# A hybrid attention and state-space layer: its instructions ordered by the scheduler with another machine model

## The chip, the cores and the metric

The kernel runs on one core of a Trainium2 chip, as one program. The metric is the device time in microseconds (us); the runs of the kernel before gave 1927.61, 1928.0 and 1932.41 us, a median of 1928.0. A core has five engines, each of which works through its own list of instructions strictly in order: TensorE (PE, with its weight loads shown apart as PEld), VectorE (DVE), ScalarE (ACT), GpSimd (POOL), and SyncE (SP), which issues the kernel's DMA transfers. Engines wait for each other by semaphores. So what an instruction waits for is not only its inputs and its buffer, but also everything that stands ahead of it in its engine's list.

## The reference

Four layers, each added to the running value `x` (4 batches of 256 tokens, 512 features, all in fp32):

```python
x = x + attention(layernorm(x))       # 32 heads of 16, rotary, causal;
                                      # plus a gated attention to 10 adapter tokens
x = x + clustered_ffn(layernorm(x))   # dense = x @ weight.T + bias, kept only where ...
x = x + mixer(layernorm(x))           # state-space layer, below
x = x + clustered_ffn(layernorm(x))   # the same weights again
```

The clustered feed-forward takes `softmax(10 * x @ centroids.T)` over 64 clusters. A token is kept when any of its clusters exceeds 0.01; a feature is kept when its cluster is hit by any token of all batches. That last condition needs every token before any token can go on.

The mixer projects 512 features to 8192 gates, 8192 channels (128 heads of 64), B and C (8 groups of 128 each) and 128 time steps `dt`. Then:

```python
xBC = silu(causal_conv4(xBC) + conv_b)
y   = sum over j <= i of (C_i . B_j) * exp(cum_i - cum_j) * dt_j * x_j   # per head
g   = (y + D * x) * silu(gate)
g   = g * rsqrt(mean(g * g over the group's 1024 channels) + eps) * norm_w
out = g @ out_w.T
```

## The kernel before, in words

**Products in three parts.** [...]

**Attention** (about 0 to 385 us). Work is done in 32 units of 4 heads (8 units for each of the 4 batches). Of a batch, queries, keys and values are prepared in steps (`prepared`, L368's neighbourhood: normalise, project, rotate), and pieces of 8 heads are made (`stacked` L305 on POOL, transposes L380, copies L382). A unit then goes through four steps, one unit apart: `scores` (products L425 and a mask product L429, row maximum L434, exponentials L437), `turn` (transposes L452, copies L453), `weigh` (four products L462 and four L468 that each write 32 partitions of one bank `py`, copy L473), and `gathered` (L479, L485). At a batch's end come `closed` (L527, L530) and `ended` (L543). The first feed-forward (`Feed`, L170 on) runs in between, a token tile at a time, its last tiles behind attention.

**The step between the layers** (about 385 to 465 us). `select` makes the mask of features out of the hits of all tokens; `take` (L229) applies it; each of the 8 token tiles is normalised (`mxn`), transposed and split into `mx`, the mixer's input. The projection to `dt`, its softplus and its running sums in chunks of 128 tokens follow. The sums are written to HBM (`cumd`) and turned (`col_t`, `dt_t`).

**The mixer's blocks** (about 465 to 1853 us). 64 blocks of 128 channels (2 heads), 8 blocks to a group. A block i goes through these steps, in the order of the source:

- the projection of its channels, `pp` (128 x 1024, two banks of PSUM, two such buffers, L676), 24 products for block and gate each; its weights come as `wr` (three buffers, L684) and are split two projections ahead;
- `conv` (L839): ACT writes the accumulator from `pp` (L842), DVE adds three taps that read `pp` (L849), ACT applies silu (L853);
- for the block before: `product` (L917), 16 matmuls L923 into the one bank pair `pyy` (L675), and `gated` (L930): L933 and L936 on DVE, the spill to HBM (L938), squares on ACT (L943, L945) and their sum on POOL (L946);
- the gate's projection into the other `pp`, and its silu into `gt` (L1042; the one buffer of L1041);
- `differences` (L876) of the two heads: DVE L881, POOL's mask L885, on ACT eight exponentials of 128 x 128 (L890, L893) and one over four batches (L891), into `em` (three buffers, L878). They read the row of running sums `r`, which SP loads two heads ahead (L873, two buffers), and need the buffer that the `pyy` products of the block before read;
- `turned` (L899): transposes L908, DVE L909 into `xd`;
- `weighted` (L897): `em` times the masked C.B of the group, `gm`.

At a group's border B of the next group is projected in block 6 and C in block 7, each into a `pp` buffer like the others and each with its conv; then `scores` (L863, L867, mask product L868) makes the next `gm`. The output product of a group runs in the blocks of the next one: `recall` (L975) loads the spilled values and splits them (`gr`, `gh`), `out_weights` (L952) loads and scales the weights (`wor`, L955, L958, L959), `root` (L964) sums the squares on PE (`pqs`, L967) and takes the root on ACT (`rg`, L971), the products write `pog`, and `scaled` (L993) adds them to `x`. Thus the first group has no output products beside it, and each later group has 8 tiles of them.

The PSUM banks that are shared in turn by `trx`, `pg`, `pqs`, `pog` and others are the two buffers of tag `m` (L671).

**The end** (about 1853 to 1929 us): output products of the last group, the second feed-forward, the store.

**What sets the order.** The source gives no engine's list by hand. The body is traced once; every operation is recorded with its dependencies and buffers. A scheduler then plays the recorded program on a model of the machine: it keeps what is ready, gives each model engine its next instruction, and moves the model's clock on by the durations that the model has for it. The sequence in which this play issues the instructions becomes each engine's list on the chip. Pools of buffers (`bufs`) limit how far it runs ahead. `tc.keep_in_program_order` holds single instructions at their place in the source (L122, L955 and some in the transition); `tc.issue_after` puts the first two heads' exponentials behind the third silu. The order of one run is fixed when the program is built; nothing is reordered on the chip.

Of the kernel before, what the change touches and what calls it, by code (L numbers as in the profile page):

```python
# [21 lines left out]
B, L, C = 4, 256, 512  # L22
# [13 lines left out]
# Columns of the constant table.  # L36
# [12 lines left out]
def constants():  # L49
    """Masks, selections and rotary tables: they depend on the shapes alone."""  # L50
# [18 lines left out]
    # [token, token tile, queries or keys, cos or sin, term]  # L69
# [8 lines left out]
def hybrid_kernel(  # L78
# [23 lines left out]
    def split(hl, v, engine=nc.vector):  # L102
        """v as the sum of two parts that each fit the products' 12 bits."""
        nc.scalar.copy(hl[0], v)  # L104
        engine.tensor_tensor(hl[1], v, hl[0].bitcast(F32), ALU.subtract)  # L105

    def mm3(o, ls, rs, first=True, last=True):
        """o = the sum over k of ls[k].T @ rs[k], operands in two parts."""
        n = len(ls)
        for k in range(n):  # L110
            (lh, ll), (rh, rl) = ls[k], rs[k]
            nc.tensor.matmul(o, lh, rh, start=(first and k == 0), stop=False)  # L112
            nc.tensor.matmul(o, lh, rl, start=False, stop=False)  # L113
            nc.tensor.matmul(o, ll, rh, start=False, stop=(last and k == n - 1))  # L114

    def warmed(o, vs):
        """Products whose result nobody reads: they keep the array's clock up in a wait."""
        for v in vs:
            nc.tensor.matmul(o[:, : v.shape[1]], ones, v, start=True, stop=True)

    def primed(func):
        """Has the scalar engine load a function's table ahead of its use."""  # L122
# [3 lines left out]
    class Norm:  # L126
        """A layer's normalisation of x."""
# [32 lines left out]
        def turn(self, xn, tr, xs):  # L160
            """In two parts, features on partitions."""
# [4 lines left out]
        def turned(self, t, xn, tr, xs):  # L166
            """A token tile normalised, in two parts, features on partitions."""
# [4 lines left out]
    class Feed:  # L172
        """One clustered layer, a token tile at a time."""
# [22 lines left out]
        def tile(self, t, xs, halves):  # L196
            """What a token tile becomes where its columns are selected, and its hits."""
# [22 lines left out]
        def select(self, cnt, rows):  # L220
            """The columns of the clusters that any token hits, as a mask."""
# [10 lines left out]
    def attention(later):  # L232
        with ExitStack() as es:
# [40 lines left out]
            def rotated(pq, c, f, name):  # L274
                """Rotary embedding, tokens on partitions; f: 0 for queries, 1 for keys."""
# [14 lines left out]
            # Parts of 8 heads side by side so that one product of 48 terms carries  # L290
            # high * high + high * low + low * high.
# [19 lines left out]
            # Adapter keys and values, spread to block diagonals.  # L311
# [7 lines left out]
            def adapter_weights():  # L319
# [9 lines left out]
                for q in range(4):  # L329
# [4 lines left out]
                    # The heads' columns: two more to the right in each of the four products.  # L334
# [22 lines left out]
            def prepared(b):  # L357
                """Steps that make a batch's queries, keys and values."""
# [12 lines left out]
            def pieces(b, q):  # L371
                """Queries and keys of 8 heads, on partitions of (2 heads, 64 terms)."""
# [40 lines left out]
            def scores(b, u):  # L413
                """Softmax numerators of 4 heads, rows on partitions."""
# [41 lines left out]
            def weigh(b, u, eT):  # L456
                """Weighted values, on partitions of (head, 32), then turned and normalised."""
# [32 lines left out]
            def adapted(b):  # L490
                """Steps that make the adapter's part."""
# [31 lines left out]
            def closed(b, k):  # L523
                """A block of features of a batch, done and turned."""
# [139 lines left out]
    def mixer(feed, later):  # L664
        with ExitStack() as es, ExitStack() as inner:
# [21 lines left out]
            def prepare(i):  # L687
                """The halves of the projection's block i, in the order of use."""
# [83 lines left out]
            # dt, and the running sums of dt * A within chunks of 128 tokens.  # L772
            cumd = dram.tile([H, NT], F32, name="cumd")
            # What a key token's sums turn: minus its own in the first chunk, its own in the
            # second, and the way to the end of the first.
# [18 lines left out]
            # ln(1 + e) by its series where e is small.  # L794
# [13 lines left out]
            for half in range(2):  # L808
# [3 lines left out]
                # From each token of a batch's first chunk to the chunk's end.  # L812
# [26 lines left out]
            def conv(pp, ch, tag, bufs):  # L839
                """silu of the causal convolution of a block of channels."""  # L840
# [15 lines left out]
            def scores(bt, ct):  # L856
                """Masked C.B of a group, key tokens on partitions."""
# [18 lines left out]
            def differences(h, r):  # L876
                """The decay from key to query: zero where the key is behind the query."""
# [21 lines left out]
            def turned(n, x2):  # L899
                """x * dt of a block, tokens on partitions, in two steps."""  # L900
# [29 lines left out]
            def gated(n, x2, gt, py, sq):  # L930
                """(y + D x) * gate of a block, and its squares added up."""
# [20 lines left out]
            def out_weights(g, k):  # L952
                """A block of output weights times the norm's, in halves."""
# [21 lines left out]
            def recall(g, t, half):  # L975
                """A token tile of half of a group's blocks, in halves."""
# [20 lines left out]
            # A group's blocks: B and C of the next group come behind its own.  # L997
# [110 lines left out]
            for t in range(TT):  # L1108
# [7 lines left out]
                # The table for roots comes before the one for exponentials.  # L1116
# [18 lines left out]
def arrange(inputs):  # L1135
    """The inputs as the program reads them: rows reordered, axes turned, nothing computed."""
    f = {k[3:]: np.asarray(v) for k, v in inputs.items()}

    def turned(w):
        # [features, inputs] -> [input in block, block of inputs, features]  # L1140
# [15 lines left out]
    # [block, feature, input block, input] -> [block, input, input block, feature]  # L1156
# [47 lines left out]
```

## Time and profile before

| | |
|---|---|
| median of the runs | 1928.0 us |
| profiled execution, first to last instruction | 1929.2 us |
| PE busy / idle | 1882.0 us (98%) / 47 us |
| DVE, ACT, POOL busy | 1478.0 (77%), 1383.7 (72%), 346.0 us (18%) |
| DMA | 240.35 MB, mean 125 GB/s |
| mean granted TensorE clock | 0.989 of full speed |
| instructions | 29952 |

The span of the profiled execution is 1.2 us more than the median of the runs, and nothing lies around it: it is the execution's own time. In a group's line "idle before, releaser" is the engine's idle time in front of those instructions and what ended most of it. Windows of the trace give, for each engine, the busy time in a stretch with the number of instructions, then the clock granted to TensorE (1.00 is full speed), the share of time that DMA engines were busy, and GB/s. In a timeline each line is a run of like instructions: when it starts, how long it lasts, engine, source line, operation, tiles, and how many there are; a bracket at the end names an idle time ahead of it and its cause.

### The profile page before, as it was taken

How to read it: one execution, taken by the hardware profiler on the slowest of the kernel's cores; microseconds unless marked ns; L12 is line 12 of the kernel's file. 1: busy time of each engine (PE TensorE's matmuls, PEld its weight loads, DVE VectorE, ACT ScalarE, POOL GpSimd, SP SyncE). 2: the span in 40 equal slices, each digit the busy share in tenths (PEclk: the TensorE clock that was granted, in tenths of full speed). 3: DMA queues.
4: the chain of work that ended last, by engine and by line, in shares of the span. 5: the costliest groups of instructions: out<-in, count | busy, mean ns of one | idle time of the engine just before them, and what ended most of it. 6: DMA issues, size and time to landing. Idle time of an engine off the chain costs nothing.

```text
span 1929.2 us, 29952 instructions
## 1 busy us (share of the span) xinstructions
PE 1882.0 (98%) x10690; PEld 1470.6 (76%) x10690; DVE 1478.0 (77%) x2324; ACT 1383.7 (72%) x2873; POOL 346.0 (18%) x306
## 2 busy tenths in 40 slices
PE   7999999989999999999999999999999999999997
PEld 6767767767777777877787777777777777787786
DVE  5556557679998878877877797778777877877777
ACT  5665667557898677876877787778677877786753
POOL 4112120011231111122121111211111111121100
PEclk7999999989999999999999999999999999999999
DMA  4000000014555554555454455445444545455341
GB/s 140 1 1 1 1 22 24 12 38 153 166 193 182 158 166 146 154 153 164 152 164 149 154 164 160 149 144 181 148 164 151 160 157 159 133 169 158 117 126 48
DMA packets 151909, 240.35 MB, mean 125 GB/s; under 512 B 12368, under 2 KB 77520, under 8 KB 151760
## 3 DMA queue, kind: packets, MB, share of 16 engines
q1 hardware_dynamic: 151760, 238.44, 39.0%
q8 instruction: 84, 1.38, 0.3%
q14 instruction: 65, 0.53, 0.1%
HBM read 202.75 MB, written 35.65 MB: 124 GB/s over the span
## 4 chain that ended last, share of the span: by engine, by line
PE 83%; DVE 5%; ACT 5%; DMA 2%; issue 2%; SPq 0%; DVEq 0%; ACTq 0%
PE pp L112 12%; PE pp L114 12%; PE pp L113 11%; PE pyy L923 8%; PE pog L112 6%; PE pog L114 6%; PE pog L113 6%; PE sc L425 3%; PE trx L908 3%; PE ptr L452 2%; PE py L462 1%; DMA wor<-in_wout_dram 1%; PE sc L429 1%; PE trp L380 1%; DVE acc L849 1%
## 5 line engine op out<-in xcount | busy, mean ns | idle before, releaser
L112 PE MATMUL pp<-mx,w 128*128 128x512 f32 (+1 forms) x1160 | 469.1, 404 | 7.2 <-DVE acc L849 6.7
L114 PE MATMUL pp<-mx,w 128*128 128x512 f32 (+1 forms) x1160 | 459.0, 396 | 0.0
L113 PE MATMUL pp<-mx,w 128*128 128x512 f32 (+1 forms) x1160 | 458.1, 395 | 0.0
L849 DVE SCALAR_TENSOR_TENSOR acc<-pp,cw_s,acc 128x1012 f32<-128x1012 f32 (+2 forms) x240 | 304.8, 1270 | 23.7 <-ACT acc L842 23.1
L897 DVE TENSOR_TENSOR em<-em,gm 128x1536 f32<-128x1536 f32 x128 | 228.3, 1784 | 88.9 <-ACT em L891 80.6
L112 PEld LDWEIGHTS pp<-mx,w 128*128 128x128 f32 x1160 | 218.8, 189 | 68.3 <-issue 10.3
L114 PEld LDWEIGHTS pp<-mx,w 128*128 128x128 f32 x1160 | 218.6, 188 | 49.3 <-issue 0.4
L113 PEld LDWEIGHTS pp<-mx,w 128*128 128x128 f32 x1160 | 219.0, 189 | 45.1 <-issue 0.7
L946 POOL TENSOR_TENSOR sq<-sq,acc 128x1024 f32<-128x1024 f32 x55 | 132.6, 2411 | 584.0 <-ACT acc L945 584.0
L885 POOL TENSOR_SCALAR_AFFINE_SELECT r<-r 128x512 f32<-128x512 f32 x128 | 128.8, 1007 | 550.1 <-DMA r<-cumd 427.4
L104 ACT CAST w<-wr 128x512 fp32r<-128x512 f32 x144 | 88.5, 615 | 193.2 <-PE pp L113 169.9
L112 PE MATMUL pog<-wo,gh 128*128 128x512 f32 x512 | 204.2, 399 | 0.0
L114 PE MATMUL pog<-wo,gh 128*128 128x512 f32 x512 | 200.4, 392 | 0.0
L113 PE MATMUL pog<-wo,gh 128*128 128x512 f32 x512 | 199.7, 390 | 0.0
L890 ACT ACTIVATE em<-r,col_t 128x128 f32<-128x128 f32 x512 | 164.9, 390 | 48.3 <-PE pyy L923 46.9
L923 PE MATMUL pyy<-em,xd 128*64 128x256 f32 (+1 forms) x2048 | 188.7, 329 | 2.0 <-DVE em L897 1.9
L923 PEld LDWEIGHTS pyy<-em,xd 128*64 128x64 f32 x2048 | 133.1, 137 | 64.8 <-issue 21.1
L893 ACT ACTIVATE em<-r,col_t 128x128 f32<-128x128 f32 x512 | 166.4, 388 | 0.0
L881 DVE TENSOR_SCALAR em<-r,col_t 128x128 f32<-128x128 f32 x512 | 136.6, 326 | 11.8 <-PE pyy L923 10.1
L909 DVE TENSOR_TENSOR xd<-trx,dt_t 128x512 f32<-128x512 f32 x128 | 86.2, 683 | 61.6 <-PE trx L908 61.4
L105 DVE TENSOR_TENSOR w<-wr,w 128x512 fp32r<-128x512 f32 x139 | 98.0, 706 | 43.1 <-ACT w L104 42.4
L437 ACT ACTIVATE e<-sc,nmx 128x128 f32<-128x128 f32 (+1 forms) x256 | 105.4, 425 | 14.9 <-DVE nmx L434 14.8
(285 smaller groups left out, 3320.7 us busy)
## 6 DMA issues: line engine op xcount, KB each, us to landing
wr<-in_win_dram SPq DMA_DIRECT2D x287, 256.0 KB, 2.9
r<-cumd SPq DMA_DIRECT2D x128, 512.0 KB, 4.2
spill<-gb SPq DMA_DIRECT2D x63, 512.0 KB, 2.9
gr<-spill SPq DMA_DIRECT2D x120, 256.0 KB, 3.5
wor<-in_wout_dram SPq DMA_DIRECT2D x64, 256.0 KB, 3.1
out_dram<-x SPq DMA_DIRECT2D x8, 256.0 KB, 2.3
x<-in_x_dram SPq DMA_DIRECT2D x1, 1536.0 KB, 9.9
gr<-spill SPq DMA_DIRECT2D x8, 192.0 KB, 2.6
```

The source lines that it names most:

```text
L112: nc.tensor.matmul(o, lh, rh, start=(first and k == 0), stop=False)
L113: nc.tensor.matmul(o, lh, rl, start=False, stop=False)
L114: nc.tensor.matmul(o, ll, rh, start=False, stop=(last and k == n - 1))
L437: nc.scalar.activation(es_[c][:, 2 * j + pr, :], sc[:, j, :n], AF.Exp, bias=nm[:, j : j + 1], accum_out=rs[:, c, h : h + 1],)
L849: nc.vector.scalar_tensor_tensor(av[:, :, d:], pv[:, :, : L - d], cw_s[:, ch, tap : tap + 1], av[:, :, d:], ALU.mult, ALU.add,)
L881: nc.vector.tensor_scalar(e[:, b, 2, :], rv[:, b, 1, :], col_t[:, h, b, 1:2], 0.0, ALU.subtract, ALU.min,)
L885: nc.gpsimd.affine_select(rv[:, :, 0, :], rv[:, :, 0, :], pattern=[[0, B], [1, P]], compare_op=ALU.is_ge, fill=-1e30, base=0, channel_mult ...
L890: nc.scalar.activation(e[:, b, 1, :], rv[:, b, 1, :], AF.Exp, bias=col_t[:, h, b, 2:3])
L893: nc.scalar.activation(e[:, b, 0, :], rv[:, b, 0, :], AF.Exp, bias=col_t[:, h, b, 0:1])
L897: nc.vector.tensor_tensor(e, e, gm, ALU.mult)
L923: nc.tensor.matmul(py[d, b, k * P :], xd[:, 2 * b + k, d], es2[hh][:, b, 2 * k : 2 if k == 0 else 3, :].rearrange("p s i -> p (s i)"), sta ...
L946: (nc.gpsimd if n < NB - 1 else nc.vector).tensor_tensor(sq, sq, x2, ALU.add)
```

## The change

One argument of the context in which the kernel body is traced. It tells the scheduler to play the program on the machine of the timeline simulator instead of its default machine model. All computations, buffers, pools and pins stay as they are.

```diff
-    with tile.TileContext(nc) as tc:
+    with tile.TileContext(nc, schedule_with_timeline_sim=True) as tc:
         hybrid_kernel(tc, *args)
```

The rest of the diff takes comments and docstrings out, and leaves empty lines in their place, so that line numbers stay the same, for instance:

```diff
     def split(hl, v, engine=nc.vector):
-        """v as the sum of two parts that each fit the products' 12 bits."""
+
         nc.scalar.copy(hl[0], v)
```

Both programs can be set side by side before they run. They hold the same matmuls, vector operations and transfers; ACT has 195 table loads instead of 191, since the load for the silu of a block now stands ahead of L1042 in 48 places. The lists of all five engines differ. On PE, the 16 products L923 of a block stood together in 52 of 64 blocks and as 1 + 15 in 11; now they stand together in 14, as 8 + 8 in 36, and in other parts in 14. The four products L462 of an attention unit come in 32 runs instead of 55, those of L468 in 35 instead of 47, and the transposes L452 in 139 runs instead of 117. On ACT, 16 exponentials (those of both heads of a block) stand between a conv's start L842 and the next gate silu L1042 in 60 of 64 blocks; before, there were 14 to 16 in most blocks, and 8 in 14 blocks next to a group's border. On SP the loads of `wv` moved behind the large load of `x`, and up to six `wr` loads stand in a row ahead of an `r`. On POOL the mask operations L885 stand three and one around the sum L946 where they stood two and two.

## The prediction

> **What bounds the kernel now.** I read the page first, engine shares and then the costliest groups with the idle time in front of them:
>
> ```profile
> span 1929.2 us, 29952 instructions
> ...
> PE 1882.0 (98%) x10690; PEld 1470.6 (76%) x10690; DVE 1478.0 (77%) x2324; ACT 1383.7 (72%) x2873; POOL 346.0 (18%) x306
> ...
> L112 PE MATMUL pp<-mx,w 128*128 128x512 f32 (+1 forms) x1160 | 469.1, 404 | 7.2 <-DVE acc L849 6.7
> ```
>
> PE is busy 98% of the span: all its idle time is 47 us, so no order can gain more than that plus what PE wastes inside its own sequence. In the mixer its only repeated wait is a projection (`pp`) that waits for a convolution tap (L849), 6.7 us in all. Then the stretches (columns: length, PE, PEld, DVE, ACT, POOL busy with instructions, granted clock, DMA share, GB/s):
>
> ```profile
> 375.00:380.00 5.00, 2.91 (x19) 1.87 (x17) 3.75 (x13) 1.43 (x5) 0.00 (x0) 1.00 0.00 0
> 380.00:385.00 5.00, 4.61 (x15) 3.77 (x16) 0.67 (x2) 1.66 (x2) 0.00 (x0) 0.66 0.02 3
> ...
> 480.00:520.00 40.00, 38.26 (x222) 29.10 (x221) 39.15 (x50) 35.64 (x73) 9.39 (x8) 1.00 0.53 170
> ...
> 800.00:840.00 40.00, 40.00 (x220) 31.75 (x219) 30.68 (x41) 28.94 (x61) 6.21 (x5) 1.00 0.45 139
> ...
> 920.00:960.00 40.00, 39.15 (x215) 30.75 (x212) 34.31 (x46) 34.22 (x54) 4.31 (x3) 1.00 0.45 141
> ```
>
> In mid-group (800) PE never stops and ACT and DVE have a quarter of their time free. At a group's end (920) and in the first group (480, no output products yet) ACT and DVE are at 34 to 39 of 40: there the order decides. The timeline of ACT at a group's end shows the sequence that the change touches:
>
> ```profile
> 922.21 1.19 ACT L842 ACTIVATE acc<-pp,cb_s,cw_s 128x1024 f32<-128x1024 f32 x1
> 923.42 1.28 ACT L890 ACT_TABLE_LOAD   x1
> 924.71 1.28 ACT L890 ACTIVATE em<-r,col_t 128x128 f32<-128x128 f32 x4
> 925.90 0.68 ACT L893 ACTIVATE em<-r,col_t 128x128 f32<-128x128 f32 x2
> 926.48 1.05 ACT L945 ACTIVATE acc<-gb 128x1024 f32<-128x1024 f32 x1
> 927.43 0.68 ACT L893 ACTIVATE em<-r,col_t 128x128 f32<-128x128 f32 x2
> 928.13 1.28 ACT L1042 ACT_TABLE_LOAD   x1
> 929.42 1.03 ACT L1042 ACTIVATE gt<-pp 128x1024 f32<-128x1024 f32 x1
> ```
>
> Eight exponentials (L890, L893), those of one head, stand before the gate's silu (L1042), which frees a `pp` buffer. And PE there, with the one wait of 0.77 us:
>
> ```profile
> 919.71 2.55 PE L923 MATMUL pyy<-em,xd 128*64 128x256 f32 x30
> 922.20 0.50 PE L112 MATMUL pp<-mx,w 128*128 128x512 f32 x1
> ...
> 928.80 0.47 PE L112 MATMUL pp<-mx,w 128*128 128x512 f32 x1 [0.77 <-DVE acc L849]
> ```
>
> **The change part by part.** No instruction's work changes; each engine's list is reordered, SP's and POOL's too, and ACT gets 195 table loads for 191 (4 x 1.28, beside PE). I read the new order of each engine and costed it with rows of this trace; the sum starts at the profiled 1929.2 us, which lies 1.2 above the median of the runs.
>
> *Group ends, groups 2 to 8.* In the new order all 16 exponentials of a block stand between a convolution's start and the next gate silu in 60 of 64 blocks; before, it was 8 in 14 of the blocks at a group's border. At block 7 a third projection (C of the next group) follows at once and needs one of the two `pp` buffers. From the end of the x projection ACT has: cast 0.52, L842 1.21, table 1.29, 16 exponentials 4 x 1.19 = 4.76, two L891 1.08, cast 0.52, L945 0.95, table 1.29, L1042 1.03: 12.65. PE has 11 of the 16 `pyy` products (11/16 x 2.75 = 1.9, 0.4 around them) and 24 matmuls at 0.2325 (5.6): 7.9. Wait 4.7. The other buffer comes no sooner: the third tap now stands on DVE behind L881, L936 and an L897 (1.7). Everything of PE is behind this wait: C, the C.B products, the next block. Five groups show this sequence, one more place has 4.0: 27.5. The root of a group (L971) frees the bank that the first output product needs: ACT has 15 exponentials 4.4, three table loads 3.9, silu 1.0, root 0.3 = 9.6; PE has `pqs` 1.7, 24 matmuls 5.6, transposes and changes 0.7 = 8.0; wait 1.6, five times: 8. Taps: eight places of 0.9 to 1.8, because eight subtractions (0.19), L933 (1.19) and a mask product now lie between taps two and three: 9. Two places at C.B: 2. Together 46, less the 6 of before that they replace: **+40**.
>
> *First group and the dt stage (425 to 640).* No output products cover anything here and DVE is at 39 of 40. Three gate silus: 16 exponentials that wait for `pyy` to free `em` 4.76, L842 1.21, two L891 1.08, L943 0.95, table 1.29, L1042 1.03 = 10.3 against 3.2 of PE work: 7.1; the others 5.5 and 7.2. C.B: its mask product L868 stands on DVE behind the weights' L105, which waits for a cast behind two table loads and eight exponentials: 3.4; then behind L881, which waits for `r` (SP issues it behind a `wr`; 4.2 us to land, page): 3.0. `pyy` directly behind its transposes waits for L909 (2.4, 3.3, 0.9) and L897 (3.7, 1.2, 1.2). Taps 7.7. Together 48, less 4 of before: **+44**; bounds +15 (the gates alone, less what is there now) and +60.
>
> *PE's own sequence.* Before, 52 of 64 `pyy` groups run whole and 11 as 1 + 15; after, 14 whole, 36 as 8 + 8, 14 odd. A whole group takes 2.75 start to start, its batches 0.65 each, so each visit costs 0.15; a projection that starts again behind one 0.2. 117 visits for 76 and 191 projection runs for 179: 41 x 0.15 + 12 x 0.2 = **+9** (5 to 15). In attention it goes the other way: four products of L462 run side by side in 0.46, a lone one takes 0.55; before they come in 55 runs and L468 in 47 and take 41.4 us start to start, after in 32 and 35: 26.3. With 22 more runs of `ptr` transposes (0.09 each) and fewer of the rest: -16. Against it about 9 of new short waits (transposes of L380 eleven times behind their copies L382, `py` behind L473), since ACT and DVE are at two thirds there: **-7** (-16 to +5).
>
> *Start, transition, tail.* The interleaved queries and keys of two tiles save one 4 us wait for `axs`, a stack (POOL L306) costs 3 and 2, and `wv` moves on SP behind the 1.5 MB of `x` (9.9 us to land): -2 (-4 to +5). Between the layers five waits for `mxn` instead of three, more for `mx`: +6 (0 to 15). At the end `gh` and `x` 3, the count 1, the last group 1: +5 (0 to 8).
>
> *Clock.* Behind two idle stretches of 2.0 us in 377 to 380 the rows show 0.66 in the next 5 us: 1.7 us lost. Some 17 of the waits above are of 2 us or more. At the group ends the loss lets ACT catch up and eats the two later waits (1.1 + 1.6), so it costs nothing; of the 11 in the first group, 19 us, about half: **+8** (0 to 30). [...]
>
> The table load took 1.28 in every row here, and the next instruction started within 0.05. [...]
>
> Sum: 1929.2 - 2 - 7 + 6 + 44 + 40 + 9 + 5 + 8 = 2032, 2031 on the scale of the median. All low ends at once give about 1953, all high ends 2117.
>
> **The rivals.**
> - *Only the group ends wait.* The first group is DVE-bound already (39 of 40), so what PE waits there may be time that DVE would have cost anyway. Without the 44 and the 8: 1980. For it: PE waits only about 4 us there before although DVE is full. Against: DVE itself stands still 5.6 us in the C.B chain.
> - *The other side: the silu is in time.* If the 12.65 of ACT shrinks below 8.7 (7.9 plus the present 0.8), by fewer exponentials behind the x projection than the list shows because some ran during it, the group ends cost nothing, and attention's regrouping decides: 1929 - 16 + 9 - 2 = 1920, faster. Against: the exponentials of a block wait for `em` buffers that `pyy` frees after the x projection.
> - *The clock stays down.* The trace has one case where a 2.8 us idle is followed by 17 us at half clock (35 to 52 us). Five such at 8.5 us lost: 2032 + 43 - 8 = 2067 and more.
> - *It does nothing.* Excluded: the lists differ on every engine. Within 0.3% (6 us, about what a measurement of this kernel can tell) only by cancellation.
>
> **How the numbers follow.** Forecast 0.60 (1995 to 2060), only the group ends 0.20 (1960 to 1995), clock 0.13 (2060 to 2110), silu in time 0.05, cancellation 0.02. Predicted time 2031. Range 1976 to 2088: it cuts half of the second and third case and all of the last two. Faster 0.05, same 0.02, slower 0.93.
>
> **What would show it.** Right: `pp` waits for ACT `gt` L1042, some 45 us in 8 to 11 places, absent before; `pog` waits for ACT `rg`; PE idle near 150 us for 47; windows of half clock after 480 us; L462 only in fours; attention no longer than before. Wrong: if `pp` still waits for L849 alone with under 10 us, the chain of exponentials was covered; if attention ends over 15 us late, its short waits were undersized; if PE's idle is small and the time still long, the split `pyy` cost more than 0.15 a visit.

## The result, and the profile after

The changed kernel takes 2087.1 us (median of 4 runs, 2084.65 to 2087.44) against 1928.2 us before: the ratio is 1.081, with a 95% interval of 1.0794 to 1.0827. That is 159 us slower; the prediction said 103 slower, in a range that ends at 2088.

The head of the page of the changed kernel, and its group of projections, answer to the first lines shown of the kernel before:

```profile
span 2085.5 us, 29994 instructions
...
PE 1938.1 (93%) x10690; PEld 1505.2 (72%) x10690; DVE 1549.3 (74%) x2324; ACT 1385.8 (66%) x2877; POOL 403.3 (19%) x306
...
L112 PE MATMUL pp<-mx,w 128*128 128x512 f32 (+1 forms) x1160 | 478.0, 412 | 63.3 <-ACT gt L1042 51.9
```

L112, L113 and L114 are the three products that `mm3` makes of a pair of operands, each split in two by a cast (L104) and a subtraction (L105). PE's idle time went from 47 to 147 us, but its busy time also grew, by 56 us, with the same 10690 matmuls. The idle time ahead of L112 is now 63.3 us and most of it waits for the gate's silu L1042, where before it was 7.2 us and waited for a tap. The windows (columns as before) show what the busy time is made of:

```profile
480.00:520.00 40.00, 25.74 (x103) 18.94 (x104) 23.56 (x32) 23.87 (x49) 3.43 (x5) 0.71 0.32 106
800.00:840.00 40.00, 34.55 (x169) 26.77 (x164) 29.80 (x38) 27.19 (x53) 9.08 (x6) 0.91 0.43 136
920.00:960.00 40.00, 39.83 (x216) 30.75 (x215) 33.39 (x44) 30.31 (x58) 7.47 (x6) 1.00 0.46 148
```

In the first group PE is busy for 25.7 of 40 us, and the granted clock is 0.71 there; around a group's end (827 us) it is 0.91; only in mid-group, here 920 to 960, is it 1.00. A group's end on the three engines, PE first, then DVE, then ACT (timelines; the bracket is the idle time ahead and its cause):

```profile
827.08 0.40 PE L114 MATMUL pp<-mx,w 128*128 128x512 f32 x1
832.93 0.80 PE L112 MATMUL pp<-mx,w 128*128 128x512 f32 x1 [5.45 <-ACT gt L1042]
833.52 0.63 PE L113 MATMUL pp<-mx,w 128*128 128x512 f32 x1
```

```profile
826.62 1.27 DVE L849 SCALAR_TENSOR_TENSOR acc<-pp,cw_s,acc 128x1016 f32<-128x1016 f32 x1
828.58 1.76 DVE L897 TENSOR_TENSOR em<-em,gm 128x1536 f32<-128x1536 f32 x1 [0.69 <-ACT em L891]
830.26 1.27 DVE L849 SCALAR_TENSOR_TENSOR acc<-pp,cw_s,acc 128x1020 f32<-128x1020 f32 x1
```

```profile
820.73 1.20 ACT L842 ACTIVATE acc<-pp,cb_s,cw_s 128x1024 f32<-128x1024 f32 x1
821.94 1.28 ACT L890 ACT_TABLE_LOAD   x1
823.24 1.28 ACT L890 ACTIVATE em<-r,col_t 128x128 f32<-128x128 f32 x4
824.42 1.27 ACT L893 ACTIVATE em<-r,col_t 128x128 f32<-128x128 f32 x4
825.59 1.27 ACT L890 ACTIVATE em<-r,col_t 128x128 f32<-128x128 f32 x4
826.77 1.26 ACT L893 ACTIVATE em<-r,col_t 128x128 f32<-128x128 f32 x4
827.94 1.13 ACT L891 ACTIVATE em<-em 128x512 f32<-128x512 f32 x2
828.98 0.60 ACT L104 CAST w<-wr 128x512 fp32r<-128x512 f32 x1
829.49 1.05 ACT L945 ACTIVATE acc<-gb 128x1024 f32<-128x1024 f32 x1
830.56 1.28 ACT L1042 ACT_TABLE_LOAD   x1
831.85 1.02 ACT L1042 ACTIVATE gt<-pp 128x1024 f32<-128x1024 f32 x1
```

PE stops for 5.45 us, where it stopped for 0.77 before. On ACT sixteen exponentials stand ahead of L1042, as the new order had said. On DVE the third tap stands behind L897, which waits for the last exponentials. And behind the wait the products run at 0.43 us start to start instead of 0.23: the granted clock is 0.5 from 831.0 to 837.8 us.

From the two traces I split each stage's length into three parts: idle is time without a matmul record on PE; clock is half of the time that PE was busy while the granted clock was 0.5; the rest is PE's own sequence. "dt and first group" runs from the first L821 to the ninth block's first L923, "groups 2 to 8" from there to the last L967. All in us, before and after:

| stage | length | idle | clock | rest |
|---|---|---|---|---|
| start | 37.3, 39.3 | 10.3, 10.9 | 2.5, 3.9 | 24.5, 24.5 |
| attention, to the count of hits | 361.9, 375.3 | 8.7, 23.9 | 9.1, 22.0 | 344.1, 329.4 |
| between the layers | 44.8, 52.8 | 6.2, 7.7 | 4.5, 3.4 | 34.1, 41.7 |
| dt and first group | 156.8, 211.0 | 3.9, 45.4 | 0.0, 15.5 | 152.9, 150.1 |
| groups 2 to 8 | 1252.6, 1326.8 | 7.9, 44.6 | 0.0, 24.8 | 1244.5, 1257.4 |
| end | 75.8, 80.4 | 10.2, 15.0 | 0.0, 2.9 | 65.6, 62.5 |
| sum | 1929.2, 2085.5 | 47.2, 147.4 | 16.2, 72.5 | 1865.8, 1865.6 |

So 100 us are idle time, 56 us are half clock, and PE's own sequence costs the same in sum.

### The profile page after: what moved, and what is told of

It reads as the page before. It is cut to its first block, busy times and chain, and to the rows that moved or that the text cites. A ratio compares the mean times of both kernels' runs of the same rounds, so it can differ in the third digit from the quotient of the medians.

```text
span 2085.5 us, 29994 instructions
## 1 busy us (share of the span) xinstructions
PE 1938.1 (93%) x10690; PEld 1505.2 (72%) x10690; DVE 1549.3 (74%) x2324; ACT 1385.8 (66%) x2877; POOL 403.3 (19%) x306
## 4 chain that ended last, share of the span: by engine, by line
PE 58%; ACT 13%; DVE 8%; DMA 3%; issue 3%; POOL 0%; SPq 0%; ACTq 0%; DVEq 0%; POOLq 0%
PE pp L112 10%; PE pp L113 10%; PE pp L114 9%; PE pyy L923 7%; PE pog L112 5%; PE pog L114 5%; PE pog L113 5%; ACT em L893 3%; ACT em L890 2%; PE trx L908 2%; DVE em L897 2%; DVE acc L849 1%; DMA wor<-in_wout_dram 1%; ACT L890 1%; ACT em L891 1%
## 5 line engine op out<-in xcount | busy, mean ns | idle before, releaser
L112 PE MATMUL pp<-mx,w 128*128 128x512 f32 (+1 forms) x1160 | 478.0, 412 | 63.3 <-ACT gt L1042 51.9
L113 PE MATMUL pp<-mx,w 128*128 128x512 f32 (+1 forms) x1160 | 469.9, 405 | 0.0
L114 PE MATMUL pp<-mx,w 128*128 128x512 f32 (+1 forms) x1160 | 469.2, 405 | 0.0
L885 POOL TENSOR_SCALAR_AFFINE_SELECT r<-r 128x512 f32<-128x512 f32 x128 | 153.9, 1203 | 1200.2 <-DMA r<-cumd 957.8
L897 DVE TENSOR_TENSOR em<-em,gm 128x1536 f32<-128x1536 f32 x128 | 265.7, 2095 | 75.2 <-ACT em L891 75.2
L112 PEld LDWEIGHTS pp<-mx,w 128*128 128x128 f32 x1160 | 225.9, 195 | 128.9 <-ACT gt L1042 57.7
L114 PEld LDWEIGHTS pp<-mx,w 128*128 128x128 f32 x1160 | 225.4, 194 | 52.3 <-issue 2.4
L113 PEld LDWEIGHTS pp<-mx,w 128*128 128x128 f32 x1160 | 226.2, 195 | 49.6 <-issue 2.6
L923 PE MATMUL pyy<-em,xd 128*64 128x256 f32 (+1 forms) x2048 | 204.6, 339 | 14.0 <-DVE xd L909 8.6
L112 PE MATMUL pog<-wo,gh 128*128 128x512 f32 x512 | 206.0, 403 | 8.9 <-ACT rg L971 4.1
L114 PE MATMUL pog<-wo,gh 128*128 128x512 f32 x512 | 201.3, 394 | 0.1
L113 PE MATMUL pog<-wo,gh 128*128 128x512 f32 x512 | 200.8, 392 | 0.0
L105 DVE TENSOR_TENSOR w<-wr,w 128x512 fp32r<-128x512 f32 x139 | 131.8, 949 | 92.4 <-ACT w L104 86.7
L923 PEld LDWEIGHTS pyy<-em,xd 128*64 128x64 f32 x2048 | 135.7, 139 | 87.8 <-issue 32.9
L104 ACT CAST w<-wr 128x512 fp32r<-128x512 f32 x144 | 88.2, 613 | 132.5 <-PE pp L113 128.7
L853 ACT ACTIVATE acc<-acc 128x1024 f32<-128x1024 f32 x80 | 84.6, 1058 | 127.9 <-DVE acc L849 127.6
L946 POOL TENSOR_TENSOR sq<-sq,acc 128x1024 f32<-128x1024 f32 x55 | 165.6, 3011 | 14.1 <-ACT acc L945 14.1
L881 DVE TENSOR_SCALAR em<-r,col_t 128x128 f32<-128x128 f32 x512 | 114.5, 281 | 50.1 <-PE pyy L923 45.3
L105 DVE TENSOR_TENSOR gh<-gr,gh 128x512 fp32r<-128x512 f32 (+1 forms) x128 | 121.6, 954 | 20.2 <-ACT gh L104 20.2
```

The lines of the kernel that those rows point to most:

```text
L881: nc.vector.tensor_scalar(e[:, b, 2, :], rv[:, b, 1, :], col_t[:, h, b, 1:2], 0.0, ALU.subtract, ALU.min,)
L885: nc.gpsimd.affine_select(rv[:, :, 0, :], rv[:, :, 0, :], pattern=[[0, B], [1, P]], compare_op=ALU.is_ge, fill=-1e30, base=0, channel_mult ...
L897: nc.vector.tensor_tensor(e, e, gm, ALU.mult)
L923: nc.tensor.matmul(py[d, b, k * P :], xd[:, 2 * b + k, d], es2[hh][:, b, 2 * k : 2 if k == 0 else 3, :].rearrange("p s i -> p (s i)"), sta ...
L946: (nc.gpsimd if n < NB - 1 else nc.vector).tensor_tensor(sq, sq, x2, ALU.add)
```

## The experiments

In all of the edits below the body is traced twice. The first trace gives the five engines' lists as the scheduler makes them with one of the two machines. The second is held to these lists, instruction by instruction, after an edit, by edges that order issue and wait for nothing. So an experiment can move one instruction on one engine and leave every other list as it was. It does not hold which of a pool's buffers a tile gets: that follows the edited order, and it matters below. `moved(l, names, behind)` puts the named instructions directly behind another.

### The gate's silu earlier at the group ends

```diff
 # the changed kernel's lists
+for n in [8 * g + 7 for g in range(7)]:
+    # behind the block's second head, ahead of the next block's first
+    act = moved(act, [gates[n]], max(exps[8 * (2 * n + 1) : 8 * (2 * n + 2)], key=act.index))
```

> The changed kernel's five lists, with one edit in seven places: at the end of groups 1 to 7 the gate's silu (L1042) stands behind the eight exponentials of its block's second head and ahead of the eight of the next block's first head, as in the kernel before. Theory (the waits and the half clock behind them are the cost of the group ends): the five waits of 5.0 to 5.5 us for L1042 go (26 us), and with them the half-clock stretches behind them (5 events, 10.7 us lost in busy time); the two more table loads in each place take back some us at the next wait: 2048 to 2058 us, 30 to 39 less than the changed kernel's 2087. Rival (what is saved is lost again in the same group, at the root, at a tap or in the split of the weights, since ACT is behind anyway): 2070 to 2082 us.

Measured: 2104.1 us (2103.2 to 2106.1), 1.0896 times the kernel before (1.0879 to 1.0912), so slower than the changed kernel with its 1.081. The rival was nearer, and still too mild. PE and then ACT of this run at the same group's end:

```profile
841.74 0.50 PE L112 MATMUL pp<-mx,w 128*128 128x512 f32 x1 [1.67 <-ACT gt L1042]
...
851.43 1.12 PE L908 MATMUL trx<-con,acc 128*128 128x128 f32 x4 [3.86 <-ACT acc L853]
```

```profile
839.36 1.28 ACT L1042 ACT_TABLE_LOAD   x1 [1.21 <-DVE gb L936]
840.66 1.02 ACT L1042 ACTIVATE gt<-pp 128x1024 f32<-128x1024 f32 x1
841.70 1.28 ACT L890 ACT_TABLE_LOAD   x1
```

The wait for L1042 fell from 5.45 to 1.67 us, as meant. But ACT now waits 1.2 us for L936, loads two more tables, and is late for the conv's silu L853, for which the transposes wait 3.9 us. The wait changed its place: groups 2 to 7 as a whole take 1163.2 us, against 1161.4 in the changed kernel.

So the additional 17 us are not from these six places. Some 15 of them come from the first of the seven, the end of the first group: the dt stage and first group take 226.4 us for 211.0. There the changed kernel had no wait for L1042 to remove: C's projection waited 2.2 us for a tap. With the silu moved up, ACT stands still there until PE has made the gate's projection, and the exponentials behind it are late:

```profile
636.70 1.28 ACT L1042 ACT_TABLE_LOAD   x1 [11.11 <-PE pp L114]
```

### The same in the first group too

The list of blocks is `[*range(1, 8), *(8 * g + 7 for g in range(1, 7))]`.

> As the run with the group ends, and the same edit in the first group's blocks 1 to 7 too. Theory: the first group's waits for L1042 (6.4, 7.6, 8.5 and 2.2 us, 24.7 in all) shrink, with half clocks of 3.5, 3.0, 2.5 and 1.7 us behind them: another 20 to 33 us below the run with the group ends alone, near 2015 to 2035 us. Rival (the first group waits for DVE's work on the same blocks, so what the gate no longer costs is waited for at L897, L909 or a tap): less than 10 us below it.

Measured: 2127.4 us (2112.5 to 2143.0), not below the run before it but above, so neither expectation. In the dt stage and first group, against that run, the waits for L1042 fell from 25.6 to 10.6 us; those of `pyy` for L897 rose from 5.4 to 19.8, those of `pp` for taps from 11.4 to 14.8, and those of L908 for L853 from 0.4 to 5.2. The stage takes 239.0 us for 226.4. In the first group a silu that comes earlier only hands its wait on. (The profile read here is of the slowest of these runs: it lost 50 us to half clock in attention alone, whose order was not touched.)

### The next block's exponentials later

```diff
 # the changed kernel's lists, the same seven blocks
+        ...  # own, ahead: the exponentials of the block and of the next one's first head
+        late = [i for i in act[first:gate] if i not in own and i in ahead]
+        act = moved(act, late, act[end])  # behind the gate's silu and the L853 that follows
```

> The changed kernel's five lists, with one edit in the seven group ends, the mirror of the run with the gate first: the gate's silu stays where it is, and the nine exponentials of the next block's first head, which stand ahead of it, go behind it and behind the conv's silu (L853) that follows; in the changed kernel ACT is idle for some 7 us there. Theory (ACT's chain is too long by the next block's head; the silu itself can't be moved up because two more table loads and a wait for L936 then make the conv's silu late): the five waits for L1042 of 5.0 to 5.5 us shrink by 4 x 0.59 + 0.54 = 2.9 us each, 14 us, and of the 10.7 us lost to half clock behind them about half: 2064 to 2074 us. Rival (as with the gate first, the next block misses what is moved: trx, em or a tap waits instead): 2080 to 2100 us.

Measured: 2116.7 us (2113.0 to 2127.2). The waits for L1042 fell to 3.77 us only, since the cast L104 ahead of the silu waits for PE itself, and new waits came behind them: up to 5.5 us for L853 and 2.6 us at later places. That is nearer the rival, and 17 us above its range. Here too the end of the first group has the larger part: the dt stage and first group take 224.3 us for 211.0, groups 2 to 7 1167.7 for 1161.4. After these three runs, my reading that the sixteen exponentials ahead of the silu are the cause had fallen as a cause to act on: they are in the chain, but at the six later ends moving either side of it on ACT repairs nothing in sum.

### The third tap ahead of L897

C's projection can take one of two `pp` buffers: the gate's, which L1042 reads, or the channels', which the taps read. The trace above shows both to be late, the second only because L897 stands between taps two and three. Which of them C gets is settled when the program is built, not on the chip.

```diff
 # the changed kernel's lists
+for n in [8 * g + 7 for g in range(7)]:
+    ...  # mine: the conv of the block's channels
+    dve = moved(dve, taps[mine + 2 : mine + 3], taps[mine + 1])  # the third directly behind the second
```

> The changed kernel's five lists, with one edit in DVE's alone: at the end of groups 1 to 7 the third tap (L849) of the block's conv stands directly behind the second, ahead of the weighted exponentials (L897) that stood between. In the changed kernel's profile PE stops at 827.5 us, L897 waits 0.7 us for ACT's L891 and takes 1.7, the third tap ends at 831.5, and the gate's silu at 832.9. Theory (the projection of C needs the first free one of two pp buffers; both are late, and the channels' buffer is late only for L897): the tap ends at about 829.2, the wait falls from 5.0 to 5.5 us to 1.5 to 2.0, five times, and with it most of the 10.7 us of half clock: 2060 to 2072 us. Rival (C's buffer is the gate's in any case, and only the silu decides): no change, 2082 to 2090 us.

Measured: 2063.4 us (2056.3 to 2083.0), 1.0723 times the kernel before (1.0662 to 1.0784), 24 us less than the changed kernel. DVE and PE of this run at the same place:

```profile
821.21 2.58 DVE L849 SCALAR_TENSOR_TENSOR acc<-pp,cw_s,acc 128x1016 f32<-128x1016 f32 x2
823.71 1.75 DVE L897 TENSOR_TENSOR em<-em,gm 128x1536 f32<-128x1536 f32 x1
```

```profile
823.94 0.47 PE L112 MATMUL pp<-mx,w 128*128 128x512 f32 x1 [1.85 <-DVE acc L849]
```

```profile
820.00:840.00 20.00, 18.15 (x83) 14.56 (x83) 15.39 (x17) 13.29 (x22) 5.37 (x3) 1.00 0.59 174
```

```profile
825.99 1.03 ACT L1042 ACTIVATE gt<-pp 128x1024 f32<-128x1024 f32 x1
```

The wait is 1.85 us here, for the tap and no longer for the silu, and the clock stays at 1.00, where the changed kernel's window 820 to 840 has 0.83. Over groups 2 to 7, idle time fell from 40.3 to 22.1 us and clock loss from 22.2 to 12.2. Swapping one pair of instructions on DVE, at a few places, gave back what three moves on ACT could not.

The lines also show that the swap did two things. In the kernel before, C starts at 928.80, ahead of the silu at 929.42: it stands in the channels' buffer. In the changed kernel the third tap ends at 831.53, yet PE stands until the silu ends at 832.87: C stands in the gate's buffer. With the swap C starts at 823.94, right behind the tap (823.79), and the silu begins only at 825.99: C is in the channels' buffer again. So the earlier tap helps because C's buffer changed with it. That the order of the taps decides the long wait at the group ends is shown; how much is the tap's earlier end and how much the buffer was not run apart. An estimate from the changed kernel's times: in the channels' buffer, with the taps as they are, C would wait 4.1 us (827.48 to 831.53) instead of 5.45.

The same swap in all 64 blocks:

> As the run with the taps at the group ends, and the same edit for all 64 blocks. Theory (in the first group the same L897 between the taps holds up the pp buffers): 10 to 25 us below the run with the ends alone. Rival (in the first group the wait is for the gate's silu behind sixteen exponentials, which wait for the products L923 of the block before, so the tap changes nothing there): within 5 us of the run with the ends alone.

Measured: 2055.2 us (2050.1 to 2058.4). It is 8 us below, between the two expectations, and the runs overlap. The dt stage and first group take 208.0 us for 211.9 with the ends alone, which is within the rival's 5. Two of the three long waits there, 7.6 and 8.2 us for L1042, became 4.0 and 5.2 us for other releasers. So the tap is late in the first group too, but little of its 41 us of waits goes with it.

### The first group alone, and attention alone

```diff
 # the lists before; a part of the program in the changed order
+part = {i.name for i in traced[at[dts[0]] : at[gates[9]]]}
+new = iter([i for i in other[e] if i in part])
+out[e] = [next(new) if i in part else i for i in l]
```

> The kernel before, with all five lists in the changed kernel's order from the softplus of dt (L788) to the ninth block's gate, and as before elsewhere. In the two profiles that stretch takes 156.8 and 211.0 us. Theory (the first group's cost is made where it is seen): +45 to +58 us, 1974 to 1990. Rival (a good part of the 54 us comes from the order of the step between the layers, late loads above all, so with that as before the same order costs less): less than +35 us.

(`gates[9]`, counted from 0, is the tenth block's gate: the stretch ends in the second group.) Measured: 1979.2 us (1976.3 to 1982.9) with 1929.3 for the kernel before, +50. The dt stage and first group took 208.1 us, 38 of the additional time idle and 16 at half clock. The theory holds: the cost is made where it is seen, whatever the step ahead of it does, and it needs nothing of the later groups.

For attention, `part` is everything up to the first L229.

> The kernel before, with all five lists up to the first L229 in the changed kernel's order, and as before behind it. In the two profiles attention takes 361.9 and 375.3 us: 15.2 us more idle, 14.7 us less of PE's own sequence, 12.9 us more lost to half clock. Theory (the half clock there belongs to the order: its stretches of small products leave the array near the limit): +8 to +18 us, 1937 to 1947. Rival (the two half-clock stretches of 17 and 14 us are an accident of how the clock's windows fall): as likely nothing as that, so -3 to +4 us.

Measured: 1952.1 us (1946.5 to 1955.7) with 1930.7 for the kernel before, +21, more than either. The attention stage of the profile: 374.9 us, 23.9 idle, 21.3 lost to half clock; it is 13.0 of the 20.6 us by which this profile is longer than the one before, and the start is 2.2. The seven profiles that have this order of attention lost 11.7 to 50.3 us there (median 21.3), four with the order before 6.3 to 9.1 (one of them is the next experiment). So the half clock belongs to the order, and how much of it there is differs between executions. In short: the regrouping that the prediction priced at -16 us did gain 14.7, idle time took 15.2 back, and the clock made it a loss.

### Four products side by side, in the order before

```diff
 # the lists before
+for line in (462, 468):  # four for each unit
+    for u in range(0, len(v), 4):
+        own = sorted(v[u : u + 4], key=pe.index)
+        ...  # ahead: the instruction in front of the last of them
+        pe = moved(pe, own, ahead)  # where the last one stood
```

> The kernel before with PE's list edited in attention alone: the four products L462 of a unit stand together, and the four L468 too, each set where its last one stood. Theory (four products on 32 columns each run side by side, a lone one doesn't): start to start L462 and L468 take 41.4 us in the kernel before and 27.7 us in the changed one, so some 13 us less: 1912 to 1918 us. Rival (a wait for the later of their inputs, or for the bank, takes the gain): 1924 to 1930 us.

Measured: 1915.9 us (1914.7 to 1916.7), 0.9919 times the kernel before (0.9905 to 0.9934). L462 and L468 take 27.5 us start to start for 41.4, and the attention stage 347.3 us for 361.9. This is the fastest version of all, faster than both kernels: the one good thing in the changed order, taken over alone.

### The products L923 cut in two, in the order before

```diff
 # the lists before; 52 blocks whose sixteen products stood whole
+        ...  # own: the block's sixteen; at: the place of the first; full: the lines L112 to L114
+        if pe[at : at + 16] == own and all(i in full for i in pe[at + 16 : at + 19]):
+            pe = moved(pe, own[8:], pe[at + 18])
```

> The kernel before, with PE's list edited: each of the 52 whole groups of 16 products L923 that is followed by projections is cut into 8 + 8 with three projection products between. The prediction's term: 0.15 us for each more visit, so +8 us, 1935 to 1939. Rival (the cut costs nothing since the other products go on without a gap): less than +2 us.

Measured: 1965.6 us (1965.0 to 1968.1), 1.0185 times the kernel before (1.0171 to 1.0200): +36, far more than both expected. PE at one of the cuts:

```profile
817.92 1.52 PE L923 MATMUL pyy<-em,xd 128*64 128x256 f32 x16
819.38 0.50 PE L112 MATMUL pp<-mx,w 128*128 128x512 f32 x1
819.71 0.39 PE L113 MATMUL pp<-mx,w 128*128 128x512 f32 x1
819.94 0.40 PE L114 MATMUL pp<-mx,w 128*128 128x512 f32 x1
820.27 1.52 PE L923 MATMUL pyy<-em,xd 128*64 128x256 f32 x16
821.72 0.51 PE L112 MATMUL pp<-mx,w 128*128 128x512 f32 x1
```

Each half takes 1.45 us start to start, two of them 2.90 for 2.75: 0.15 for a visit, exactly the term. But the three products between take 0.89 instead of 0.70, so a cut costs 0.34, and 52 of them 18 us. Another 11.5 us are idle: `pyy` done later delays taps (waits 6.7 to 13.9 us) and L853 (0.3 to 6.8). The remaining 7 us I can't assign. The prediction had priced the restart of the projection separately (0.2, twelve times); each cut brings one, and 0.15 + 0.2 is close to the 0.34 measured.

### The clock by itself

Two probes: stretches of full products (f32r, 128 x 512), with other work between.

```python
full(180)
for work, n in ...:   # one of idle time or small products
    work(n); full(180)
```

> No part of the layer: a probe of the clock alone. TensorE runs f32r products of 128x128 by 128x512 in stretches of 180 (about 42 us), and between them one stretch of something else: idle time (a chain of 1 to 10 ACT copies, some 0.6 us each, that PE waits for), or without idle time 16 to 128 products of 128x1, fp32 transposes of 128x128, fp32 products of 32 columns by 256, of 64 columns by 256, and f32r products of 128x128. Theory of the prediction (the clock falls behind idle time alone): half clock follows the idle stretches from about 2 us on, and none of the others. Rival (the clock goes by the work that the array does in a window, whether PE is idle or busy with small products): half clock follows stretches of about 4 us and more of the products of 128x1 and of 32 columns as well, with no idle time ahead, and not those that keep the array full.

> No part of the layer: the probe of the clock again, with the forms that stood in attention where the clock fell without idle time of note (two waits of 0.38 us): f32r products of 64 rows, fp32 of 80 rows, f32r of 80 columns, bf16, f32r transposes, the mixture of L425 and L429, that stretch as a whole with no, one or two short waits, short waits of about 0.7 us with three full products between, and 8 to 16 products of 128x1. Theory (only idle time and products of one column count as no work): half clock behind 128x1 products of over 2.5 us and behind none of the others; the short waits lower it only where idle time fills most of a window of 3.4 us. Rival (each form counts by the share of the array's rows, columns and moving elements that it uses): half clock behind the 64-row, 80-row or bf16 stretches as well.

Idle time first, as one stretch of waiting for ACT: 0.7 and 1.4 us did not lower the clock, 2.0 us did in three of four cases, 2.7 us in one of four, 3.3 us and more in all six. Rows of 2 to 16 waits of 0.7 us, with full products between, did so in none of six cases.

Windows of the first probe: products of 128 x 1 (516 to 530 and 571 to 598), of 32 columns (858 to 865.6) and of 64 columns (1740 to 1753):

```profile
516.00:530.00 14.00, 14.00 (x57) 12.84 (x57) 0.00 (x0) 0.00 (x0) 0.00 (x0) 0.51 0.01 1
571.00:598.00 27.00, 27.00 (x116) 25.84 (x116) 0.00 (x0) 0.00 (x0) 0.00 (x0) 0.50 0.00 1
858.00:865.60 7.60, 7.60 (x132) 4.26 (x130) 0.00 (x0) 0.00 (x0) 0.00 (x0) 1.00 0.01 2
1740.00:1753.00 13.00, 13.00 (x124) 8.67 (x122) 0.00 (x0) 0.00 (x0) 0.00 (x0) 1.00 0.01 1
```

PE's records fill all of each window, yet the granted clock is 0.51 and 0.50 in the first two. In both probes the clock fell in all six stretches of 128 x 1 products that lasted over 3.8 us, in one of two that lasted 2.4 us, and in none of two that lasted 1.5 us. Transposes and products of 32 columns, 64 columns, 64 rows, 80 rows, 80 columns and in bf16, each form by itself, did not lower it (1.00 in the last two windows). Windows of the second probe, f32r products of 64 rows (L425) and bf16 products (L429) in turn, two and one:

```profile
803.80:814.00 10.20, 10.20 (x29) 6.63 (x29) 0.00 (x0) 0.00 (x0) 0.00 (x0) 0.50 0.01 2
...
923.30:967.50 44.20, 44.20 (x127) 25.98 (x127) 0.00 (x0) 0.00 (x0) 0.00 (x0) 0.50 0.00 0
```

Each of the two forms alone kept the clock at 1.00 for 7 to 14 us; in turn they run at half clock from 3.3 to 5.5 us behind their start until behind their end, with no idle time in the records. But the records may hide some: at full clock two products of 64 rows and one in bf16 take 0.64 us start to start in turn, and alone 0.12 + 0.12 + 0.11 = 0.35. Whether TensorE stands still at each change of form, so that this is idle time again, is not shown. The mixture is the pattern of attention's scores. The copy of attention's stretch of small products fell in two of three cases with two short waits in it, in none of three with one and in none of two with none. So no expectation came out whole: half clock followed one-column products (0.50), against the first theory; it did not follow 32 columns, 64 rows, 80 rows and bf16 by themselves, against both rivals; and the mixture ran at 0.50, which the second theory excluded.

For idle time I counted in the traces of eleven runs of whole kernels (the two kernels and nine of the runs above). In those of the two kernels the half-clock stretches (6 and 26) lasted 3.41, 6.83, 10.24, 13.65 or 17.07 us, multiples of 3.41, but for the last of each, which goes on past the last instruction. So each trace was cut on that grid into pieces of 3.41 us, with products of one column counted as idle time. For pieces that were themselves at full clock:

| idle in a piece of 3.41 us | pieces | the next one at half clock |
|---|---|---|
| below 0.25 us | 5226 | 0 |
| 0.25 to 0.75 | 362 | 8 |
| 0.75 to 1.25 | 192 | 9 |
| 1.25 to 1.75 | 121 | 14 |
| 1.75 to 2.25 | 68 | 55 |
| above 2.25 | 113 | 113 |

Of the pieces already at half clock with 0.75 us or more of idle time, 88 of 88 were followed by another. On this grid a single wait of 2.7 us can be shared out between two pieces, which fits its one case of four in the probes.

## Why the prediction was right or wrong

By its own terms, with the three parts of the table above (us):

| term | forecast | measured |
|---|---|---|
| group ends, groups 2 to 8 | +40 | +36.7 (idle) |
| first group and dt stage | +44 | +41.5 (idle) |
| PE's own sequence, mixer | +9 | +10.1 (rest: -2.8 in the first group, +12.9 later) |
| attention | -16 + 9 | -14.7 (rest) + 15.2 (idle) |
| start, transition, end | -2 + 6 + 5 | +11.4 (idle and rest) |
| clock | +8 | +56.3 |

The measured time is 0.9 us inside the range and far outside the case that the prediction held likeliest (1995 to 2060): the range holds because it had been opened for the rival with the clock, not because the sum was right.

**Right: the waits.** Five group ends wait 4.96 to 5.45 us where the sum said 4.7; PE's idle time is 147 us where it said "near 150"; `pp` waits for L1042 for 51.9 us at 9 places where it said some 45 in 8 to 11; `pog` waits for `rg`. In the first group the parts agree too: silus 22.4 us for 19.8, `pyy` 12.7 for 12.7, taps 6.4 for 7.7, C.B 3.5 for 6.4 (these parts of the prediction add up to 46.6, where it wrote 48). At the group ends the total owes something to chance: the root's wait was 4.1 us for 8 and the taps 3.2 for 9, and 6.5 us of other waits, mostly for L909 and `gh`, filled the gap. In attention the sign "no longer than before" failed: it took 375.3 us for 361.9, with 15.2 us of new idle time where the prediction had 9. One detail was misread: the sixteen exponentials are not a block's two heads but the second head of a block and the first of the next; the count and the durations are the same.

**Right, but not the lever.** The sentence "The other buffer comes no sooner: the third tap now stands on DVE behind L881, L936 and an L897 (1.7)" was the more useful half of that step. Edits of the silu's place and of the exponentials' gained nothing at the later group ends and cost 13 to 15 us at the first; one swap on DVE, by which C also got the other buffer, took 24 us off.

**Wrong: the clock.** The step that failed is "At the group ends the loss lets ACT catch up and eats the two later waits (1.1 + 1.6), so it costs nothing; of the 11 in the first group, 19 us, about half: **+8** (0 to 30)". Measured, the clock costs 24.8 us in groups 2 to 8, 15.5 in the first group and 12.9 more in attention, where the step had nothing. Half-clock stretches went from 6 to 26. Four things were missing. Each group-end wait is followed by 3.4 to 6.8 us of half clock, which cost 1.5 to 2.7 us, and of the later waits that this was to eat some were still there (2.0 and 1.6 us for `rg`). A half-clock stretch of 13.7 us (677 to 691), behind the last wait of the first group, reaches into the second, with sixteen of the root's one-column products in it, and costs 6.4 us. The root's products of one column, which now follow `pyy` at once, stand ahead of a half-clock stretch with hardly any idle time (882 us: 0.08 in the 3.41 us before). And in attention, among its regrouped small products, the same happened at 203 and 292 us:

```profile
196.00:203.00 7.00, 6.23 (x57) 5.01 (x55) 2.08 (x3) 3.48 (x8) 2.15 (x3) 1.00 0.01 2
203.00:220.00 17.00, 17.00 (x77) 11.81 (x76) 7.28 (x14) 11.92 (x44) 2.74 (x7) 0.50 0.00 1
```

There 0.77 us of idle time in 7 us came ahead of 17 us at half clock with PE always busy. That this clock belongs to attention's new order is shown by the run with attention alone; which of its products or waits does it is not. The rival "the clock stays down" (2067 and more, 0.13) was thus the nearest of the cases, with another mechanism than it gave: many short stretches, not a few long ones.

The prediction's row (2.0 us idle, then 0.66) pointed the right way: more than 2.25 us of idle time in a piece of 3.41 us were followed by half clock in 113 of 113 cases, 1.75 to 2.25 us in 55 of 68. The failure was not in expecting half clock behind idle time but in where its cost was counted.

**The rivals.** "Only the group ends wait" is excluded by the run with the first group alone (+50 us). "The silu is in time" did not happen. One term came out right (+10.1 for +9) though its parts may not have: the run with the cut products shows that a cut costs 0.34 us on PE, and 0.7 us in all there. The prediction's 41 more visits at 0.34 would be 14; why the changed kernel shows less was not tested.

**Open.** Which order within the first group would remove its 41 us was not found: an earlier silu only moved the wait, and an earlier tap took 4 us off. C's buffer was not changed by itself. How much of attention's 15 us of new idle time belongs to which wait was not tested.

## What to carry to other kernels

Where a change makes waits, price the clock as a term of its own, place by place, with what the traces at hand show: here half clock followed 3.41 us with over 2.25 us of idle time, one-column products counted in, in 113 of 113 cases, and cost 1.5 to 2.7 us behind each group-end wait. Dense runs of small mixed products deserve the same suspicion (here 17 us at 0.50 behind 0.77 us of idle time). When a wait names one releaser, look for the other resource that would have served, see what delays that, and which of the two the program was given: here the cure was on DVE, though every wait named ACT. When an edit at several places gives one number, look at each place: one of seven made the first edits look harmful, at the others they did nothing. And a scheduler's order need not be taken or left as a whole: holding one list and moving one pair shows which part is worth having (attention's fours, 0.8% faster alone).

## What the runs showed of the hardware that was not expected

- In a stretch of 24.5 us of products of 128 x 1, with PE always busy in the records, all but the first 2.9 us ran at 0.50.
- f32r products of 64 rows and bf16 products in turn ran at 0.50 for 41 of 47 us without idle time in the records, while each form alone kept 1.00 for 7 to 14 us.
- Pieces of 3.41 us with 1.75 to 2.25 us of idle time were followed by half clock in 55 of 68 cases, and those with 0.25 to 1.75 us in 31 of 675, where the prediction had counted waits from 2 us on.
- The same order of attention lost 11.7 to 50.3 us to half clock in seven profiles; whole runs with it spread by up to 30 us, where those of the kernel before spread by 6.
